# Key weights of a graph attention layer: 13 bursts of 768 columns a head over six PSUM banks, instead of 20 bursts of 475 or 494 over four

## The chip, the cores and the metric

One core of a Trainium2 chip runs the kernel. It has a matrix engine (PE, with its weight loads listed apart as PEld), three elementwise engines (DVE, ACT, POOL), a queue engine (SP) that issues most DMAs, an on-chip memory SBUF of 128 partitions, and a matmul memory PSUM of eight banks, each 128 partitions by 512 f32. The metric is device time in microseconds (us). All arithmetic here is in f32.

## The reference

A layer of two-direction graph attention over B = 16 batches of N = 512 nodes with F = 512 features, H = 16 heads of dh = 32, and only the first NG = 20 nodes as keys. Cut to what matters:

```python
vcq = concatenate([v, where(row_zero, 0, q)])          # (16, 512, 1024)
self_feat = vcq @ W_self.T + b_self                    # (16, 512, 512)
output = self_feat
for d in range(2):                                     # adjacency, and its transpose
    A = (adj if d == 0 else swapaxes(adj, 1, 2))[:, :, :20, :]
    cond, vb = A.sum(-1), A @ w_bias + b_bias          # 11 labels
    kv = self_feat[:, :20]
    qh = (self_feat @ Wq[d].T + bq[d]).reshape(B, N, 16, 32)
    kh = (kv @ Wk[d].T + bk[d]).reshape(B, 20, 16, 32)
    aff = einsum('bnhd,bmhd->bnhm', qh, kh) / sqrt(32)
    w = softmax(where(cond > 0, aff, -9e15) + vb)      # over the 20 keys
    out_t = einsum('bnhm,bmf->bnhf', w, kv)
    output += einsum('bnhf,hgf->bnhg', out_t, Wout[d]) + bout[d]
return v + relu(output)
```

## The kernel before, in words

The kernel never forms `qh`. Scores of a batch are one product of `self_feat` with **key weights** g: for each head and key, Wq of that head times the key's row. A softmax doesn't change when one key's score is taken from all of them, so only ND = 19 differences of keys are kept for each batch, direction and head. The program has a setup (everything for all 16 batches that depends on the keys), a loop over batches from L1085, and a tail from L1293.

**Setup.** Self features of the keys come first (L781), their differences `kvD` (L821, on DVE) and key rows `khD` (`key_rows`, matmul L838, then L847 on DVE), one for each direction d and group hg of four heads. Then come the **bursts** (`keys`, matmul L937). A unit is one batch of 19 columns, for a block fc of 128 features, a group hg, a direction d. A burst takes 26 or 25 units in order, so 494 or 475 columns, and cuts them into runs wherever fc, hg or d changes. Each run is one matmul for each of the four heads hl of the group. Such a matmul contracts over the 32 rows of its head, so the four heads sit in four row groups of the array and run side by side. Each head has a PSUM bank of its own: heads 0 and 1 in the pair of banks s0, heads 2 and 3 in the pair s1. ACT empties s0 (L959) and DVE s1 (L961), one instruction for a run, both with the scale, into stage tiles `st` (one per fc and hg: 128 by batch, head, direction, key). When a stage tile is full, POOL copies batch 0 into `g0` (L965), which the loop's first batch reads, and SP stores the other 15 batches to `g_d` in DRAM (L968). The loop reads a batch's key weights back with four loads (`load_keys`).

Between two bursts PE works on **fillers**, so that ACT and DVE have time to empty the banks. A string `plan` (L990) says which fillers follow which burst: `v` and `w` (`values`, L900, products of key features with Wout), `c` (`bias_scores`, L873), `n` (`row_flags`, L220, which rows are zero), `p` (`block_product`, L282, the first batch's self features); `m` and `b` are work for DVE and ACT. Early bursts have `key_rows` there instead. Fillers use a rotating pool of four banks, s0 and s1 the other four. Each engine runs its own instructions in the order in which the program is written.

**Loop.** For each batch, halves, directions and row blocks go through `score_product` (L395), mask and softmax (ACT, DVE, POOL: `weigh`, `lowered`, `total`, `normal`), a transpose (`turn`, DVE L543) and `attend` (L567 on PE). `normal` multiplies by the reciprocal sum (POOL L535), `key_sum` forms differences of key weights for products that serve several blocks (POOL L368), `apart` builds a part of the values (POOL L167), `mask_spread` and `mask_count` prepare masks (L344, L331).

Of the kernel before, what the change touches and what calls it, by code (L numbers as in the profile page):

```python
# [7 lines left out]
F32 = mybir.dt.float32  # L8
# [5 lines left out]
P = 128  # L14
# [4 lines left out]
def gat_kernel(  # L19
# [47 lines left out]
    def bank(name):  # L67
        return acc["pool"].tile([P, 512], F32, tag="acc", name=name)
# [10 lines left out]
    g0 = const.tile([P, C, WD], F32, tag="g", name="g0")  # L79
# [7 lines left out]
    g_d = dram.tile([C * C, P, B - 1, WD // C], F32, name="g_d")  # L87
# [44 lines left out]
    def load_keys(b, ks=range(C), ins=None):  # L132
        if ks[0] == 0:
            gs[b] = (gp if b % 2 else const).tile([P, C, WD], F32, tag="g", name=f"g{b}", bufs=1)
        src = g_d[:, :, b - 1]
# [81 lines left out]
    def row_flags(b):  # L217
        ps = bank(f"ps_nz{b}")
        for a in range(HL):
            nc.tensor.matmul(ps[bass.ts(a, R), :N], ones[:, :R], rss[b], start=True, stop=True)  # L220
        nzs[b] = load.tile([P, N], F32, tag="nz", name=f"nz{b}")
        nc.vector.tensor_scalar(nzs[b], ps[:, :N], 0.0, None, ALU.not_equal)
# [34 lines left out]
    def product(b, n):  # L257
# [13 lines left out]
        if first:  # L271
            parts[b, home] = bank(f"ps_{home}{b}")
# [424 lines left out]
    with tc.tile_pool(name="setup", bufs=1) as sp, tc.tile_pool(name="ps_acc", bufs=4, space=PSUM) as acc["pool"]:  # L697
        wq_sb = sp.tile([P, 2, C, F], F32, name="wq_sb")
        wo_sb = sp.tile([P, 2, C, F], F32, name="wo_sb")
# [16 lines left out]
        with tc.tile_pool(name="setup_k", bufs=1) as sk:  # L716
# [17 lines left out]
            warm = bank("ps_warm")  # L734
# [32 lines left out]
            nc.sync.dma_start(bb_sb, b_bias.partition_broadcast(P))  # L767
            for d in range(2):
                rows(wo_sb[:, d], woT[d])
            load_x(1)  # L770
            load_adj(0, 1)
# [5 lines left out]
            kv_ps = [bank(f"ps_kv{fc}") for fc in range(C)]  # L777
# [32 lines left out]
            for fc in range(C):  # L810
# [11 lines left out]
                    kvD[:, fc].rearrange("p (b m) -> p b m", m=ND), each[:, :, 1:],  # L822
# [8 lines left out]
            def key_rows(d, jc, ks=range(C)):  # L831

                if ks[0] == 0 and (d, jc) not in of:
                    of[d, jc] = bank(f"ps_k{d}{jc}")
# [32 lines left out]
        with tc.tile_pool(name="setup_g", bufs=3) as sg:  # L867

            def bias_scores(d):

                ps = bank(f"ps_c{d}")
                for c in range(C):
# [7 lines left out]
                    ps[:, : B * ND].rearrange("p (b m) -> p b m", m=ND),  # L880
# [10 lines left out]
            def values(t, ds, k):  # L891
# [3 lines left out]
                if k == 0:  # L895
                    held[1 + t // 2] = bank(f"ps_v{t}{ds[0]}")
                ps = held[1 + t // 2]
                for i, d in enumerate(ds):
                    for a in range(rows // R):
                        nc.tensor.matmul(  # L900
                            ps[bass.ds(i * rows + a * R, R)], kvT[:, k, bass.ds(t * P + a * R, R)], wo_sb[:, d, k],
# [26 lines left out]
            def keys(runs):  # L928


                pairs = [ps_s.tile([P, 2, 512], F32, tag=f"s{i}", name=f"ps_g{runs[0]}{i}", bufs=1) for i in range(2)]
                at = 0
                for fc, hg, d, lo, hi in runs:
                    n = (hi - lo) * ND
                    for hl in range(HL):
                        r = bass.ts(hl, DH)
                        nc.tensor.matmul(  # L937
                            pairs[hl // 2][:, hl % 2, at : at + n], wq_sb[r, d, hg, bass.ts(fc, P)],
                            khD[r, d * C + hg, lo * ND : hi * ND], start=at == 0, stop=True, skip_group_check=True,
                        )  # L940
                    at += n
                if not units and runs is bursts[-1]:
                    for hl in range(HL):
                        r = bass.ts(hl, DH)
                        nc.tensor.matmul(
                            pairs[hl // 2][:, hl % 2, at:], wq_sb[r, 0, 0, :P], khD[r, 0, : 512 - at],
                            start=False, stop=True, skip_group_check=True,
                        )
                at = 0
                for fc, hg, d, lo, hi in runs:  # L950
                    n = (hi - lo) * ND
# [10 lines left out]
                    at += n  # L962
                    if d == 1 and hi == B:
                        to, of = g0[:, fc, bass.ts(hg, WD // C)], st[:, 0].rearrange("p h d m -> p (h d m)")
                        nc.gpsimd.tensor_copy(to, of)  # L965
                        to, of = g_d[C * fc + hg], st[:, 1:].rearrange("p b h d m -> p b (h d m)")
                        most = fc * hg < (C - 1) * (C - 1)
                        nc.sync.dma_start(*((to, of) if most else (to[:, :1], of[:, :1])))  # L968
# [25 lines left out]
            while units:  # L994
                runs = []
                for fc, hg, d, b in units[: 25 + (len(bursts) % 5 < 3)]:
                    if runs and runs[-1][:3] == (fc, hg, d):
                        runs[-1] = (*runs[-1][:4], b + 1)
                    else:
                        runs.append((fc, hg, d, b, b + 1))  # L1000
                del units[: 25 + (len(bursts) % 5 < 3)]
                bursts.append(runs)
            rest = [(d, hg) for hg in range(C) for d in range(2)]
            first = None
# [8 lines left out]
            for n, runs in enumerate(bursts):  # L1013
                for i in range(len(rest)):
                    if (i < 1 and n > 0) or any(fc == 0 and (d, hg) == rest[0] for fc, hg, d, _, _ in runs):
                        key_rows(*rest.pop(0))
                if n in (3, 4):
                    values(*steps["v"].pop(0)[1])
                if n == 0:
                    bo_rows = load.tile([P, C, N], F32, tag="x2", name="bo_rows", bufs=1)  # L1020
                    nc.sync.dma_start(bo_rows[:, :2], bout.partition_broadcast(P))
                keys(runs)
                if n == 8:
                    mask_count(0, 0)
                if n == 14:
                    mask_count(0, 1)
                if n == 17:
                    mask_sum(0, 1)
                value_pieces()
                if rest:  # L1030
                    for kind in "mm" if n else ():
                        f, args = steps[kind].pop(0)
                        f(*args)
                    continue
                if n == 7:
                    mask_mul(0, 0)
                first = n if first is None else first
# [395 lines left out]
```

## Time and profile before

| what | value |
|---|---|
| median of 3 runs | 547.67 us (547.23 to 548.54) |
| the profiled execution | 547.91 us |
| span of its trace | 546.2 us |
| first burst, first score product of the loop | 24.26 us, 89.17 us |
| POOL, DVE, ACT busy, share of the span | 82%, 88%, 74% |

A row of the timeline or the groups reads: start and duration in us, or a count, then engine, line and operation, output <- inputs, partitions x elements. `32*128` before a matmul's shape is the part of the array it uses, rows times columns. An f32 matmul leaves two records, one for each of two passes. The profile's span is 1.7 us shorter than the time of the execution that it belongs to.

### The profile page before, as it was taken

How to read it: one execution, taken by the hardware profiler on the slowest of the kernel's cores; microseconds unless marked ns; L12 is line 12 of the kernel's file. 1: busy time of each engine (PE TensorE's matmuls, PEld its weight loads, DVE VectorE, ACT ScalarE, POOL GpSimd, SP SyncE). 2: the span in 40 equal slices, each digit the busy share in tenths (PEclk: the TensorE clock that was granted, in tenths of full speed). 3: DMA queues.
4: the chain of work that ended last, by engine and by line, in shares of the span. 5: the costliest groups of instructions: out<-in, count | busy, mean ns of one | idle time of the engine just before them, and what ended most of it. 6: DMA issues, size and time to landing. Idle time of an engine off the chain costs nothing.

```text
span 546.2 us, 19863 instructions
## 1 busy us (share of the span) xinstructions
PE 539.6 (99%) x8012; PEld 421.6 (77%) x8012; DVE 481.3 (88%) x716; ACT 404.6 (74%) x1000; POOL 449.5 (82%) x454
## 2 busy tenths in 40 slices
PE   8999999999999999999999999999999999999996
PEld 5544368889788878787888878888878788878784
DVE  1776678889999999999999999999998999999997
ACT  1225445888787979788888888888878887978564
POOL 2647995779989897979898989898998989797675
PEclk9999999999999999999999999999999999999998
DMA  8999899967676777787776867676777776736025
GB/s 312 378 401 347 280 370 359 321 193 215 200 223 181 226 204 208 240 214 227 214 215 188 229 186 214 212 199 216 193 240 191 219 211 184 233 95 192 2 65 195
DMA packets 96715, 122.80 MB, mean 225 GB/s; under 512 B 19264, under 2 KB 65022, under 8 KB 94576
## 3 DMA queue, kind: packets, MB, share of 16 engines
q1 hardware_dynamic: 95200, 119.18, 70.6%
q0 software_dynamic: 992, 1.57, 1.4%
q8 instruction: 63, 1.03, 0.8%
q10 hardware_dynamic: 432, 0.79, 0.4%
q14 instruction: 28, 0.23, 0.1%
HBM read 84.66 MB, written 38.15 MB: 225 GB/s over the span
## 4 chain that ended last, share of the span: by engine, by line
PE 90%; DVE 3%; DMA 2%; ACT 2%; POOL 1%; issue 1%; DVEq 0%; ACTq 0%; POOLq 0%
PE ps_f L665 29%; PE ps_a L395 22%; PE ps_c L395 10%; PE ps_d L395 6%; PE ps_o_f L567 5%; PE ps_v L900 3%; PE ps_k L838 3%; PE ps_kv L781 2%; PE ps_a L282 1%; PE ps_o_c L567 1%; PE ps_l L395 1%; DMA nz_d<-nz 1%; DMA nz<-nz_d 1%; PE ps_c L282 1%; DMA ws_v<-in_wsT 1%; DVE sm L530 1%
## 5 line engine op out<-in xcount | busy, mean ns | idle before, releaser
L325 ACT ACTIVATE prod<-adj,wb_sb 128x80 f32<-128x80 int32 x330 | 116.1, 430 | 0.0
L535 POOL TENSOR_TENSOR w<-w,sm 128x640 f32<-128x640 f32 x63 | 80.4, 1276 | 30.9 <-DVE sm L531 27.5
L665 PE MATMUL ps_f<-t,ws_s 128*64 128x246 f32 x720 | 80.0, 370 | 0.0
L665 PEld LDWEIGHTS ps_f<-t,ws_s 128*64 128x64 f32 x720 | 51.7, 136 | 18.9
L526 ACT ACTIVATE w<-w 128x640 f32<-128x640 f32 x60 | 43.9, 731 | 18.5 <-DVE w L522 18.5
L543 DVE STREAM_TRANSPOSE wt<-w 128x640 f32<-128x640 f32 x63 | 52.5, 834 | 0.9 <-POOL w L535 0.8
L665 PE MATMUL ps_f<-x,ws_v 128*64 128x246 f32 x480 | 52.4, 371 | 0.0
L530 DVE TENSOR_REDUCE sm<-w 128x32 f32<-128x640 f32 x63 | 51.1, 811 | 1.2 <-ACT w L526 1.0
L521 DVE TENSOR_REDUCE ps_d<-w 128x32 f32<-128x640 f32 x59 | 48.7, 826 | 1.8 <-ACT ps_d L429 0.2
L522 DVE TENSOR_TENSOR w<-w,ps_d 128x640 f32<-128x640 f32 x59 | 48.4, 821 | 2.0
L665 PEld LDWEIGHTS ps_f<-x,ws_v 128*64 128x64 f32 x480 | 34.7, 137 | 13.0
L368 POOL TENSOR_TENSOR k<-g,k 128x608 f32<-128x608 f32 x30 | 44.6, 1488 | 0.0
L395 PEld LDWEIGHTS ps_a<-g,sf 128*64 128x64 f32 x544 | 34.2, 137 | 5.9 <-issue 5.8
L395 PE MATMUL ps_a<-g,sf 128*64 128x152 f32 x544 | 38.6, 295 | 0.0
L395 PE MATMUL ps_d<-g,sf 128*64 128x152 f32 x544 | 37.9, 293 | 0.0
L336 DVE TENSOR_REDUCE add<-prod 128x80 f32<-128x960 f32 x32 | 36.7, 1146 | 0.8 <-POOL prod L331 0.7
L344 ACT COPY both<-add 64x80 f32<-64x80 f32 x128 | 32.7, 255 | 5.7 <-DVE add L336 4.6
L567 PE MATMUL ps_o_c<-wt,ve 32*32 32x256 f32 (+1 forms) x480 | 35.9, 386 | 0.0
L680 POOL TENSOR_TENSOR t<-x,t 128x492 f32<-128x492 f32 x30 | 34.8, 1160 | 1.2
L395 PEld LDWEIGHTS ps_d<-g,sf 128*64 128x64 f32 x544 | 35.3, 137 | 0.2 <-ACT sf L683 0.2
L680 POOL TENSOR_TENSOR t<-x 128x492 f32<-128x492 f32 x30 | 34.5, 1150 | 0.0
L197 ACT ACTIVATE xn<-xn 128x512 f32<-128x512 f32 x56 | 34.5, 619 | 0.0
(308 smaller groups left out, 1487.7 us busy)
## 6 DMA issues: line engine op xcount, KB each, us to landing
g<-g_d SPq DMA_DIRECT2D x60, 304.0 KB, 3.1
g_d<-st SPq DMA_DIRECT2D x15, 1140.0 KB, 8.2
out_T<-o SPq DMA_DIRECT2D x64, 256.0 KB, 3.3
x<-in_xT SPq DMA_DIRECT2D x56, 256.0 KB, 4.3
xn<-in_xn SPq DMA_DIRECT2D x48, 256.0 KB, 5.4
adj<-in_adj SPq DMA_DIRECT2D x52, 220.0 KB, 3.6
nz<-nz_d SPq DMA_DIRECT2D x14, 256.0 KB, 5.3
adj<-in_adj SPq DMA_DIRECT2D x6, 440.0 KB, 5.8
```

Source lines behind the costliest of these rows:

```text
L325: nc.scalar.activation(p[:, :, l], a[:, :, l], AF.Identity, scale=wb_sb[:, l : l + 1])
L368: done["ksum"] = engine.tensor_sub(to, one, two)
L395: nc.tensor.matmul(slot(g)[bass.ts(p, P // 2), : HL * S].rearrange("p (h m) -> p h m", m=NG)[:, :, 1:], of(k)[:, bass.ds(first + g * P // ...
L521: nc.vector.tensor_reduce(mx, f, AX.X, ALU.max)
L522: done["weigh"] = (engine or nc.vector).tensor_sub(f, f, mx.unsqueeze(2).to_broadcast([P, per, NG]))
L526: done["exp"] = nc.scalar.activation(t, t, AF.Exp)
L530: nc.vector.tensor_reduce(sm, heads(weighs[b, c, l]), AX.X, ALU.add)
L535: done["normal"] = nc.gpsimd.tensor_mul(f, f, smalls.pop((b, c, l)).unsqueeze(2).to_broadcast([P, per, NG]))
L543: done["turn"] = nc.vector.transpose(wts[b][:, c, l], weighs.pop((b, c, l)).rearrange("p g w -> p (g w)"))
L567: nc.tensor.matmul(outsum[b][a][bass.ds(at // 2 * DH, n * DH), bass.ds(c * N // 2 + lo * R, (hi - lo) * R)].rearrange("p (n r) -> p n r", ...
L665: nc.tensor.matmul(parts[b][n in (2, 3, 5)][bass.ts(a, P // 2), bass.ts(i, HN)], lhs, x[:, k], start=False, stop=k == 1, skip_group_check= ...
L680: done["xsum"] = nc.gpsimd.tensor_sub(to, one, two)
```

## The change

- **Units, bursts, banks.** A unit is now one key for all 16 batches: 16 columns of `khD`, whose columns are now ordered key first, batch second (`kvD` is written in that order, L821). A burst takes 48 units, 768 columns a head; there are 13 (the last has 32 units). The first 32 units fill the banks s0 and s1 as before. The other 16 ("more") go to a third tile `both` of two banks, t2: heads 0 and 1 share its first bank, 256 columns each, heads 2 and 3 its second. Fillers have two banks, acc0 and acc1.
- **Order in a burst.** Heads 0 and 2 begin with their runs in t2, heads 1 and 3 end with them. The second head of a bank waits for the first one's matmul.
- **Emptying.** ACT still takes the half of heads 0 and 1, DVE the other one, now of s0, s1 and of both banks of t2. The innermost loop of these instructions is the batch, which is the outermost in `st`, so consecutive elements lie 608 bytes apart (4 heads x 2 x 19 x 4 bytes); before, 19 consecutive elements lay side by side. The third tile is read by ACT and DVE in turns, as the second listing below shows.
- **Plan.** `plan` is new: up to three `v` after a burst. `values` and `row_flags` use 64-column tiles in place of 32-column ones, half the instructions. The extra matmuls L945 at the end of the last burst are gone.
- **Batch 1.** POOL copies batch 1 too, into `g1` (16 copies more); `g_d` has 14 batches, and the four loads of batch 1 are gone, as is the late store at L1141. The second half of Wout lies in the buffer that `ws_q` frees.
- **Loop, batch 1.** In that batch alone, `apart` comes earlier and one `key_sum` of batch 2 later.

```diff
-            def keys(runs):
-                pairs = [ps_s.tile([P, 2, 512], F32, tag=f"s{i}", name=f"ps_g{runs[0]}{i}", bufs=1) for i in range(2)]
+            def keys(n):
+                runs = bursts[n]
+                pairs = [ps_s.tile([P, 2, 512], F32, tag=f"s{i}", name=f"ps_g{n}{i}", bufs=1) for i in range(2)]
+                both = acc["pool"].tile([P, 2, 512], F32, tag="t2", name=f"ps_g{n}2") if n + 1 < len(bursts) else None
+                each = [sorted(runs, key=lambda run: hl % 2 == (run[5] > 0)) for hl in range(HL)]
+                gone = [0] * HL
+                while any(each):
+                    hl = min((hl for hl in range(HL) if each[hl]), key=lambda hl: gone[hl])
+                    fc, hg, d, lo, hi, more, at = each[hl].pop(0)
...
+                    to = both[:, hl // 2, bass.ds(hl % 2 * 256 + at, w)] if more else pairs[hl // 2][:, hl % 2, bass.ds(at, w)]
+                    if more and hl % 2 and at == 0:
+                        behind(nc.tensor.nop(), done["key", hl - 1])
...
-                        to = st[:, lo:hi, bass.ts(half, 2), d].rearrange("p b h m -> p h b m")
-                        of = pairs[half][:, :, at : at + n].rearrange("p h (b m) -> p h b m", m=ND)
+                        to = st[:, :, bass.ts(half, 2), d, lo:hi].rearrange("p b h m -> p h m b")
+                        of = both[:, half].rearrange("p (h w) -> p h w", h=2) if more else pairs[half]
+                        of = of[:, :, bass.ds(at, (hi - lo) * B)].rearrange("p h (m b) -> p h m b", b=B)
...
-            plan = "mmvv bvv vvc vvc vvn vvw vw vw wn p p p p p p p".split()
+            plan = "mm mmm mmmvvv vvv vvvb cvvv vvc vvn wwwn wp pp pp pp".split()
...
-            units = [(fc, hg, d, b) for fc in range(C) for hg in range(C) for d in range(2) for b in range(B)]
+            units = [(fc, hg, d, m) for fc in range(C) for hg in range(C) for d in range(2) for m in range(ND)]
...
-                    if d == 1 and hi == B:
-                        to, of = g0[:, fc, bass.ts(hg, WD // C)], st[:, 0].rearrange("p h d m -> p (h d m)")
-                        nc.gpsimd.tensor_copy(to, of)
+                    if d == 1 and hi == ND:
+                        for b in range(2):
+                            nc.gpsimd.tensor_copy(
+                                near[b][:, fc, bass.ts(hg, WD // C)], st[:, b].rearrange("p h d m -> p (h d m)")
+                            )
+                        nc.sync.dma_start(g_d[C * fc + hg], st[:, 2:].rearrange("p b h d m -> p b (h d m)"))
...
             if more:
-                at(further, key_sum, b + 1, 1)
+                at(b == 1, apart, 0)
+                at(b != 1 and further, key_sum, b + 1, 1)
                 mask_spread(b + 1, 0)
                 mask_count(b + 1, 1)
...
-            at(b == 1, apart, 0)
             total(b, 1, 1)
             at(0 < b and further, load_nz, b + 2, done["sum"])
             normal(b, 1, 1)
+            at(b == 1, key_sum, 2, 1)
```

On PE, the second burst before (`ps_g...0` and `...1` are the pairs s0 and s1; the last number of a shape is the columns of the run) was issued like this:

```order
L937 MATMUL ps_g(0, 0, 1, 10, 16)0_408<-khD_101,wq_sb_99 128x114 [waits PE_49,Activation_49]
L937 MATMUL ps_g(0, 0, 1, 10, 16)0_408<-khD_101,wq_sb_99 128x114
L937 MATMUL ps_g(0, 0, 1, 10, 16)1_409<-khD_101,wq_sb_99 128x114 [waits DVE_49,PE_49]
L937 MATMUL ps_g(0, 0, 1, 10, 16)1_409<-khD_101,wq_sb_99 128x114
L937 MATMUL ps_g(0, 0, 1, 10, 16)0_408<-khD_101,wq_sb_99 128x304 x2
L937 MATMUL ps_g(0, 0, 1, 10, 16)1_409<-khD_101,wq_sb_99 128x304 x2
L937 MATMUL ps_g(0, 0, 1, 10, 16)0_408<-khD_101,wq_sb_99 128x76 x2
L937 MATMUL ps_g(0, 0, 1, 10, 16)1_409<-khD_101,wq_sb_99 128x76 x2
```

The fourth burst after (numbered 3; `ps_g30` and `ps_g31` are the pairs, `ps_g32` is t2) begins like this:

```order
L943 MATMUL ps_g32_582<-khD_102,wq_sb_100 128x224 [waits DVE_49,PE_49]
L943 MATMUL ps_g30_580<-khD_102,wq_sb_100 128x128
L943 MATMUL ps_g32_582<-khD_102,wq_sb_100 128x224
L943 MATMUL ps_g31_581<-khD_102,wq_sb_100 128x128
L943 MATMUL ps_g30_580<-khD_102,wq_sb_100 128x304
L943 MATMUL ps_g31_581<-khD_102,wq_sb_100 128x304
L943 MATMUL ps_g32_582<-khD_102,wq_sb_100 128x32 x2
L943 MATMUL ps_g30_580<-khD_102,wq_sb_100 128x128
L943 MATMUL ps_g31_581<-khD_102,wq_sb_100 128x128
```

The first matmul of a burst now writes t2, and it is the one that waits for DVE; before, the first ones wrote the pairs and waited for ACT and for DVE, each for its own pair.

On ACT, the same burst is emptied with these five instructions:

```order
L958 ACTIVATE st03_556<-ps_g30_580 128x2x8x16 [waits PE_49]
L958 ACTIVATE st10_610<-ps_g30_580 128x2x19x16 [waits DMAHW3_49,Activation_49,Pool_49]
L958 ACTIVATE st10_610<-ps_g30_580 128x2x5x16
L958 ACTIVATE st10_610<-ps_g32_582 128x2x14x16 [waits PE_49]
L958 ACTIVATE st11_620<-ps_g32_582 128x2x2x16 [waits DMAHW4_49,DVE_49,Pool_49]
```

and on DVE with these:

```order
L960 TENSOR_SCALAR st03_556<-ps_g31_581 128x2x8x16 [waits PE_49]
L960 TENSOR_SCALAR st10_610<-ps_g31_581 128x2x19x16 [waits DMAHW3_49,Pool_49]
L960 TENSOR_SCALAR st10_610<-ps_g31_581 128x2x5x16
L960 TENSOR_SCALAR st10_610<-ps_g32_582 128x2x14x16 [waits Activation_49]
L960 TENSOR_SCALAR st11_620<-ps_g32_582 128x2x2x16 [waits DMAHW4_49,Activation_49]
```

Emptying the pairs needs no turn of the other engine. For t2, DVE's first piece waits for ACT's first, ACT's second for DVE's first, and DVE's second for ACT's second.

On POOL, these rows stood in the last part of batch 1 in the loop (the digit behind a letter is the batch: `k2_1` and `g2` are of batch 2, `w1_11` and `sm1_11` of batch 1, `ve0` and `vd0` the values of batch 0):

```order
L368 TENSOR_TENSOR k1_2_1486<-g1_1174,k1_2_1486 128x608
L368 TENSOR_TENSOR k2_1_1727<-g2_1490 128x608 [waits DMAHW7_49,DMAHW2_49,PE_49]
L331 TENSOR_SCALAR prod2_1_1672<-cond2_1_1733 128x80 [waits DVE_49]
L167 TENSOR_TENSOR ve0_1740<-vd0_1577,own_85 128x192 [waits DMAHW5_49,DMAHW6_49,DMAHW4_49,DMAHW3_49]
L167 TENSOR_TENSOR ve0_1740<-vd0_1577,own_85 128x192
L535 TENSOR_TENSOR w1_11_1660<-w1_11_1660,sm1_11_1743 128x640 [waits DVE_49,Activation_49]
```

and after the change these:

```order
L368 TENSOR_TENSOR k1_2_1520<-g1_85,k1_2_1520 128x608
L167 TENSOR_TENSOR ve0_1761<-vd0_1611,own_86 128x192 [waits DMAHW2_49,DMAHW7_49,DMAHW1_49,DMAHW0_49]
L167 TENSOR_TENSOR ve0_1761<-vd0_1611,own_86 128x192
L331 TENSOR_SCALAR prod2_1_1706<-cond2_1_1768 128x80 [waits DVE_49]
L535 TENSOR_TENSOR w1_11_1694<-w1_11_1694,sm1_11_1775 128x640 [waits DVE_49,Activation_49]
L368 TENSOR_TENSOR k2_1_1781<-g2_1524 128x608 [waits DMAHW6_49,DMAHW3_49,PE_49]
```

The row `k2_1` has moved from ahead of `w1_11` to behind it, and the two rows `ve0` stand ahead of `prod2_1`.

More of the change, by code (lines that the diff above doesn't have):

```diff
@@ L217, in row_flags @@
     def row_flags(b):
-        ps = bank(f"ps_nz{b}")
-        for a in range(HL):
-            nc.tensor.matmul(ps[bass.ts(a, R), :N], ones[:, :R], rss[b], start=True, stop=True)
+        ps = bank(f"ps_nz{b}", 1)
+        for a in range(2):
+            nc.tensor.matmul(ps[bass.ts(a, P // 2), :N], ones[:, : P // 2], rss[b], start=True, stop=True)
         nzs[b] = load.tile([P, N], F32, tag="nz", name=f"nz{b}")
@@ new lines, in keys @@
+            def keys(n):
[7 more added lines that the diff above has]
+                    fc, hg, d, lo, hi, more, at = each[hl].pop(0)
+                    r, w = bass.ts(hl, DH), (hi - lo) * B
+                    gone[hl] += w
+                    to = both[:, hl // 2, bass.ds(hl % 2 * 256 + at, w)] if more else pairs[hl // 2][:, hl % 2, bass.ds(at, w)]
+                    if more and hl % 2 and at == 0:
+                        behind(nc.tensor.nop(), done["key", hl - 1])
+                    one = nc.tensor.matmul(
+                        to, wq_sb[r, d, hg, bass.ts(fc, P)], khD[r, d * C + hg, lo * B : hi * B],
+                        start=at == 0 and not (more and hl % 2), stop=True, skip_group_check=True,
+                    )
+                    if more:
+                        done["key", hl] = one
+                for fc, hg, d, lo, hi, more, at in runs:
@@ L1163, in gat_kernel @@
                 total(b, 0, 0)
-                at(more, load_keys, b + 1, range(2, 3), done["sum"])
+                at(one and more, load_keys, b + 1, range(2, 3), done["sum"])
                 normal(b, 0, 0)
@@ L1173, in gat_kernel @@
                 normal(1, 0, 0)
-            at(more, load_keys, b + 1, range(3, 4), done["sum" if b == 1 else "lowered"])
+            at(one and more, load_keys, b + 1, range(3, 4), done["sum" if b == 1 else "lowered"])
             at(two, turn, b - 1, 0, 1)
```

174 lines of the change are left out of this document (70 added, 104 removed).

## The prediction

> **What bounds the kernel now.** I read the head of the page first, then the slices, then the chain that ended last.
>
> ```profile
> span 546.2 us, 19863 instructions
> PE 539.6 (99%) x8012; PEld 421.6 (77%) x8012; DVE 481.3 (88%) x716; ACT 404.6 (74%) x1000; POOL 449.5 (82%) x454
> PE   8999999999999999999999999999999999999996
> PEclk9999999999999999999999999999999999999998
> PE 90%; DVE 3%; DMA 2%; ACT 2%; POOL 1%; issue 1%; DVEq 0%; ACTq 0%; POOLq 0%
> ```
>
> PE is busy 99% of the span, at full clock in nearly every slice, and holds 90% of the chain. So time goes only if PE gets less work or loses a gap, and time comes whenever another engine makes PE wait. Next I cut the span into the stretch of the bursts and the loop's batches 0 to 2.
>
> ```profile
> 24.30:89.20 64.90, 64.87 (x841) 33.91 (x838) 46.59 (x92) 28.09 (x67) 45.71 (x64) 1.00 0.98 350
> 89.20:115.30 26.10, 26.10 (x337) 22.49 (x338) 22.96 (x27) 19.98 (x52) 22.37 (x20) 1.00 0.80 275
> 115.30:144.80 29.50, 29.41 (x434) 25.26 (x430) 27.55 (x41) 25.38 (x64) 26.14 (x26) 1.00 0.80 230
> 144.80:173.40 28.60, 28.60 (x440) 23.60 (x432) 26.97 (x39) 24.37 (x63) 25.72 (x25) 1.00 0.71 209
> ```
>
> Columns: window, length, then busy time of PE, PEld, DVE, ACT, POOL, then clock, DMA share, GB/s. In the stretch of the bursts PE never waits (64.87 of 64.90), so nothing is hidden there for the change to uncover: it can only shorten PE's work, or break a cover that holds today. Batch 1 is 0.9 us longer than batch 2, and 0.09 of it is idle time.
>
> **The change part by part.** First PE's work in the setup. The first row below is the same cut for the lines of the bursts alone, the others are PE's timeline (start, length):
>
> ```profile
> 24.20:89.20 65.00, 23.12 (x384) 15.76 (x384) 1.00 0.98 350
> ...
> 43.02 1.92 PE L900 MATMUL ps_v<-wo_sb,kvT 128*32 128x512 f32 x16
> 44.87 0.37 PE L937 MATMUL _g(1, 0, 1, 10, 16)0_609<-khD,wq_sb 32*128 32x114 f32 x2
> ...
> 45.99 1.92 PE L900 MATMUL ps_v<-wo_sb,kvT 128*32 128x512 f32 x16
> ...
> 83.09 0.28 PE L937 MATMUL g(3, 2, 0, 14, 16)0_1047<-khD,wq_sb 32*128 32x38 f32 x2
> ...
> 83.20 0.50 PE L937 MATMUL g(3, 2, 0, 14, 16)0_1047<-khD,wq_sb 32*128 32x304 f32 x2
> ```
>
> The 20 bursts are 23.12 us busy, their overlapping ends counted; from start to start, as in 44.87 to 45.99, one takes 1.01 to 1.18, and 20 take 21.9. The columns are 9728 a head (12 x 494 + 8 x 475). A column costs 1.67 ns in two passes: a burst of 304 + 190 columns without a short run takes 1.05 = 0.82 + 0.22 of switching. 9728 columns take 16.2 us, before and after. A short pass does not shrink with its columns: the pass of 38 columns takes 83.20 - 83.09 = 0.11, where its columns alone would take 0.03. Runs under 134 columns lose about 0.11 - 0.83 ns x columns in each pass. Before there are 16 of these, 1.2 us lost in all; 16.2 + 1.2 + 20 x 0.22 = 21.8 checks. After there are 22, of 16 to 128 columns, 1632 together: 22 x 0.224 - 1632 x 1.67 ns = 2.2 us. So 13 bursts take 16.2 + 2.2 + 13 x 0.22 = 21.3, with the dummy matmuls L945 gone: **-0.5 us**. A filler stretch has such a cost too:
>
> ```profile
> 56.87 2.78 PE L900 MATMUL ps_v<-wo_sb,kvT 128*32 128x512 f32 x24
> 59.58 0.53 PE L937 MATMUL s_g(2, 0, 0, 0, 16)0_773<-khD,wq_sb 32*128 32x304 f32 x2
> ```
>
> Three `v` take 59.58 - 56.87 = 2.71, two take 44.87 - 43.02 = 1.85; so one is 0.86 and each stretch has 0.14 on top. Seven stretches fewer: **-1.0 us**. The 64-column tiles of `values` I cost at nothing: the 32-column ones run side by side in the array (4 of them, 0.86 us), and half as many of double width fill it the same way. If tiles of 64 columns did not, the 16 `v` and 4 `w` would grow; nothing in the rows speaks for it, since L282 uses 64-column tiles and keeps PE full.
>
> Next, the cover. PE may start a burst when its banks are empty.
>
> ```profile
> 43.24 1.08 ACT L959 ACTIVATE st<-s_g(1, 0, 0, 0, 16)0_576 128x608 f32<-128x608 f32 x2 [1.98 <-POOL g L965]
> 43.35 1.25 DVE L961 TENSOR_SCALAR st<-s_g(1, 0, 0, 0, 16)1_577 128x608 f32<-128x608 f32 x2 [0.54 <-PE s_g(1, 0, 0, 0, 16)1_577 L937]
> L959 ACT ACTIVATE st<-_g(0, 0, 1, 10, 16)0_408 128x608 f32<-128x608 f32 x1 | 0.7, 693 | 0.0
> L959 ACT ACTIVATE st<-_g(0, 0, 1, 10, 16)0_408 128x152 f32<-128x152 f32 x1 | 0.3, 303 | 0.0
> L961 DVE TENSOR_SCALAR st<-_g(0, 0, 1, 10, 16)1_409 128x608 f32<-128x608 f32 x1 | 0.8, 782 | 0.0
> L961 DVE TENSOR_SCALAR st<-_g(0, 0, 1, 10, 16)1_409 128x152 f32<-128x152 f32 x1 | 0.3, 306 | 0.0
> ```
>
> That burst ended at 43.02; ACT began 0.22 later, and both engines had emptied the banks by 44.60, before PE's next burst at 44.87. Now ACT costs about 0.17 us + 0.86 ns an element of a partition (303 at 152, 693 at 608), DVE 0.15 + 1.04 ns. After the change a burst has 1024 elements in the pairs and 512 in t2 for each engine. On ACT the pairs end 0.22 + 1.12 = 1.34 after the burst (1.08 for 988 elements, so 1.12 for 1024). DVE empties its pair beside that. Then come the turns in t2: ACT, DVE, ACT, DVE. They are two ACT pieces, 2 x 0.17 + 512 x 0.86 ns = 0.78, two DVE pieces, 2 x 0.15 + 512 x 1.04 ns = 0.83, and four hand-overs of 0.02 to 0.1: together some 1.8. So the next burst may start **3.1 to 3.3 us** after the last one; I take 3.2. Where DVE has a `v` to add first it is later still. If the two engines needed no turns, each would be done by about 2.2.
>
> The cover after the change, by the plan, in the same rows and these:
>
> ```profile
> 25.30 2.25 PE L838 MATMUL ps_k<-kvD,wk 128*32 128x304 f32 x32
> ...
> 48.46 0.46 PE L937 MATMUL s_g(1, 1, 1, 4, 16)0_655<-khD,wq_sb 32*128 32x228 f32 x2
> ...
> 53.14 1.92 PE L900 MATMUL ps_v<-wo_sb,kvT 128*32 128x512 f32 x16
> 54.88 1.04 PE L220 MATMUL ps_nz<-rx,ones 128*32 128x512 f32 x8
> 55.85 0.41 PE L937 MATMUL s_g(1, 3, 0, 7, 16)0_739<-khD,wq_sb 32*128 32x171 f32 x2
> 78.28 1.88 PE L282 MATMUL ps_a<-t,ws_s 128*64 128x246 f32 x16
> ...
> 80.10 0.46 PE L937 MATMUL _g(3, 1, 1, 4, 16)0_1015<-khD,wq_sb 32*128 32x228 f32 x2
> ```
>
> `vvn` covers 55.85 - 53.14 = 2.71, `p` 80.10 - 78.28 = 1.82, so `wp` 0.86 + 1.82 = 2.7 and `pp` 3.5; `vvv` covers 2.71; `vvc` is the least, as before 45.99 to 48.46, 2.47. Behind bursts 0 and 1 stand two `key_rows` each (2 x 2.2, L838). So PE waits about 0.5 behind bursts 2, 3, 4, 7 and 9, 0.7 behind 6, and not behind 5, 8, 10, 11: **+3.2 us**. The waits stand at the head of PE's queue, so all fillers and the loop behind them move by as much.
>
> POOL gets 16 copies more:
>
> ```profile
> L965 POOL COPY g<-st 128x152 f32<-128x152 f32 x16 | 5.8, 369 | 12.8 <-ACT st L959 7.2 <-DVE st L961 5.6
> L331 POOL TENSOR_SCALAR prod<-cond 128x80 f32<-128x80 f32 x32 | 18.1, 565 | 8.3 <-DVE cond L330 6.6
> ```
>
> They cost 16 x 0.37 = 5.9 us on an engine that is busy 45.71 of these 64.90. POOL also builds inputs of `p`, and now seven `p` stand behind four bursts instead of seven. I put **+0.5 us** there (between 0, if they fit in its idle time, and 5.9, if all of it came late). The dropped store and loads of batch 1 take DMA traffic away (share 0.98 in this stretch); no PE wait hung on it, so nothing for that.
>
> Last, the loop's batch 1, in the chain of waits:
>
> ```profile
> 137.42 0.57 POOL prod L331
> ...
> 138.07 0.98 POOL ve L167 x2
> 139.05 1.24 POOL w L535
> ...
> 140.32 0.85 DVE wt L543
> ...
> 142.40 0.40 PE ps_o_f L567
> ```
>
> PE's `attend` at 142.40 hung on DVE's transpose, that on POOL's `w`, and that on POOL's row ahead of it. The change puts the `key_sum` of batch 2 (1.5 us, L368, before 137.42) behind `w`. Then `w` comes up to 1.5 us earlier; DVE, in order, is free for the transpose 0.8 earlier. Batch 1 exceeds batch 2 by 0.9, so I take **-0.7 us** (between 0 and -0.9). Next in line is DVE's own work.
>
> Sum against the profiled execution: 547.9 - 0.5 - 1.0 + 3.2 + 0.5 - 0.7 = **549.4**. That execution is 0.2 over the median shown, so a median may come 0.2 lower.
>
> **The price of the stride.** The emptying now writes elements 608 bytes apart. No row of ACT or DVE before shows that from PSUM; the nearest by kind is L959 itself, and the sum takes its rate. The other bound is a row that steps through SBUF, reading every 44 and writing every 48 bytes, beside one that does neither:
>
> ```profile
> L325 ACT ACTIVATE prod<-adj,wb_sb 128x80 f32<-128x80 int32 x330 | 116.1, 430 | 0.0
> L344 ACT COPY both<-add 64x80 f32<-64x80 f32 x128 | 32.7, 255 | 5.7 <-DVE add L336 4.6
> L626 ACT ACTIVATE ps_f<-nz,qw x30: 469/470/472, 90.0 to 491.1; 128x246 f32<-128x246 f32 x30
> ```
>
> L325 takes 430 ns against 255. Some 90 is its scale from memory (L626, with one too, takes 470 at 246 elements, where 0.17 + 0.86 ns gives 0.38). The other 85 over 80 elements is 1.1 ns each: the rate about halved. Read or write, the row does not tell. The Trainium skill, "SBUF — State Buffer", in the box on SBUF cachelines in the section "Door 1: The DMA port swizzle", says that memory lines are 16 bytes and that an access to a new line each time pays a penalty, four f32 being free; L325 agrees, but its read steps too. By that page the sum would be that of the rival below.
>
> **The rivals.** *Half rate.* If the stride doubles the time of an element, the chain of 3.2 grows by 1024 x 0.86 on ACT's pairs, 512 x 0.86 and 512 x 1.04 in t2: 1.8, so 5.0. Against covers of 2.5 to 3.6, ten waits sum to 20, the first two to 1; with -1.5 and -0.7 that is **567**. For it speaks L325, and L331 above, which writes every 48 bytes and takes 565 on POOL for 80 elements; against it, that L325 also reads with a step. Half of that surcharge gives 557.
> *It fits (the other side).* If the turns overlap, or a DVE or ACT piece starts while the other still reads, the banks are empty by 2.2 to 2.6 and no wait is left: 547.9 - 1.5 - 0.7 = **545.7**. It decides at 2.7, the length of `vvv`. For it: today's emptying has a margin, 44.60 against 44.87. Against it: the waits in the program name the other engine at each piece of t2.
> *Only half of it.* With waits of 0.2 in place of 0.5 and no late POOL, the parts cancel: 547.9 - 1.5 + 1.4 - 0.7 = **547.1**.
>
> **How the numbers follow.** The forecast, turns at full rate, gets 0.38 (own range 548.3 to 551.5), of which 0.05 lies under the bound; half rate or part of it 0.27 (556 to 567.5); all hidden 0.25 (545 to 546.4); cancelled 0.1. A measurement of this kernel can tell about 0.2%, 1.1 us, from no change. So faster 0.27 (all hidden, with some of the cancelled), same 0.13, slower 0.6. The range is 545.2 to 567: hidden at its low end, the doubled stride at its upper one.
>
> **What would show it.** The rows of L958 and L960: 0.69 and 0.78 us for 608 elements at full rate, 1.2 and 1.4 at half. In the timeline, PE idle ahead of L943, released by DVE, about 0.5 us, behind the bursts named. In t2 the pieces ACT, DVE, ACT, DVE one after another. PE's time from first burst to first score product: 64.9 before, about 67 if I am right, 63.4 if all is hidden, 84 at half rate. Batch 1 of the loop 28.8 in place of 29.5. Wrong would I be if pieces of t2 run side by side, or if the chain is under 2.7.

## The result

The changed kernel takes 588.71 us (median of 4 runs, 587.45 to 589.84), the kernel before 547.53 us in the same runs: a ratio of 1.075, 95% interval 1.0733 to 1.0766. It is slower, as forecast, but by 41 us and not by 2, and the time lies above the range given (545.2 to 567.0).

The head of the page of the changed kernel, and its slices:

```profile
span 585.7 us, 19799 instructions
PE 549.8 (94%) x7980; PEld 433.5 (74%) x7980; DVE 507.0 (87%) x724; ACT 434.6 (74%) x1008; POOL 452.2 (77%) x470
PE   9975686779999999999999999999999999999995
PEclk9989978989999999999999999999999999999998
```

PE has fallen from 99% to 94%, and only in slices 3 to 9. In the same slices the granted clock drops to seven to nine tenths. The first score product of the loop now starts at 128.1 us in place of 89.2, so 38.9 us of the 39.5 by which the span grew lie ahead of it.

The stretch of the bursts, cut as before (window, length, busy time of PE, PEld, DVE, ACT, POOL, then clock, DMA share, GB/s):

```profile
24.60:128.30 103.70, 75.44 (x811) 43.61 (x809) 74.00 (x100) 58.38 (x75) 50.47 (x83) 0.90 0.67 235
```

It was 64.90 long with 64.87 of PE. So PE now waits 103.70 - 75.44 = 28.3 us, and is busy 10.6 us longer, at a mean clock of 0.90: e4 below does the same work in 65.70 us at full clock. What PE waited for there (total, times, longest):

```profile
PE ps_g L943 <- DVE st L960: 21.7, 9, 3.2
PE ps_g L943 <- DVE khD L847: 3.0, 2, 2.1
PE ps_a L282 <- DVE sf L295: 2.9, 1, 2.9
PE ps_c L873 <- ACT bqbd L863: 0.7, 1, 0.7
```

The waits are of the kind that the prediction named, ahead of the bursts and for DVE. But there are nine of 1.8 to 3.2 us, 21.7 in all, where it had six of 0.5 to 0.7, 3.2 in all, and they stand behind bursts 5, 8 and 10 too, where it had none. The other three are work of DVE or ACT that stands in their queues behind the emptying. The groups of the emptying, by shape (busy, mean ns, idle before):

```profile
L958 ACT ACTIVATE st<-ps_g 128x608 f32<-128x608 f32 x8 | 14.1, 1762 | 6.7 <-PE ps_g L943 6.7
L958 ACT ACTIVATE st<-ps_g 128x32 f32<-128x32 f32 x2 | 0.6, 313 | 1.4 <-DVE st L960 1.4
...
L960 DVE TENSOR_SCALAR st<-ps_g 128x608 f32<-128x608 f32 x8 | 13.6, 1705 | 1.0 <-PE ps_g L943 1.0
...
L960 DVE TENSOR_SCALAR st<-ps_g 128x32 f32<-128x32 f32 x2 | 0.5, 232 | 0.3 <-ACT st L958 0.3
```

608 elements take 1762 ns on ACT and 1705 on DVE; they took 693 and 782. From 32 to 608 elements that is (1762 - 313) / 576 = 2.5 ns an element on ACT and (1705 - 232) / 576 = 2.6 on DVE, where 0.86 and 1.04 held before.

One burst, number 2, in the timelines of PE, ACT and DVE:

```profile
41.42 1.85 PE L943 MATMUL ps_g<-khD,wq_sb 32*128 32x80 f32 x32 [0.82 <-DVE khD L847]
43.20 2.80 PE L900 MATMUL ps_v<-wo,kvT 128*64 128x512 f32 x12
49.21 1.92 PE L943 MATMUL ps_g<-khD,wq_sb 32*128 32x224 f32 x40 [3.21 <-DVE st L960]
...
43.29 3.08 ACT L958 ACTIVATE st<-ps_g 128x576 f32<-128x576 f32 x3 [2.74 <-PE ps_g L943]
46.99 1.03 ACT L958 ACTIVATE st<-ps_g 128x352 f32<-128x352 f32 x1 [0.62 <-DVE st L960]
...
46.40 0.55 DVE L960 TENSOR_SCALAR st<-ps_g 128x160 f32<-128x160 f32 x1 [0.21 <-ACT st L958]
48.05 1.02 DVE L960 TENSOR_SCALAR st<-ps_g 128x352 f32<-128x352 f32 x1 [1.10 <-ACT st L958]
```

The burst ends at 43.20. ACT empties its pair and its first piece of t2 until 46.37, DVE takes a piece from 46.40, ACT one from 46.99, DVE the last from 48.05 to 49.07, and PE goes on at 49.21: 6.0 us after the burst, with 2.8 us of cover. The turns are as forecast; the pieces are too long.

### The profile page after: what moved, and what is told of

The parts are those of the page before. It is cut to its first block, busy times and chain, and to the rows that moved or that the text cites. A ratio compares the mean times of both kernels' runs of the same rounds, so it can differ in the third digit from the quotient of the medians.

```text
span 585.7 us, 19799 instructions
## 1 busy us (share of the span) xinstructions
PE 549.8 (94%) x7980; PEld 433.5 (74%) x7980; DVE 507.0 (87%) x724; ACT 434.6 (74%) x1008; POOL 452.2 (77%) x470
## 3 DMA queue, kind: packets, MB, share of 16 engines
q1 hardware_dynamic: 93088, 116.69, 63.4%
## 4 chain that ended last, share of the span: by engine, by line
PE 76%; DVE 2%; ACT 1%; issue 0%; DVEq 0%
PE ps_f L665 30%; PE ps_a L395 22%; PE ps_c L395 11%; PE ps_d L395 6%; PE ps_o_f L567 5%; PE ps_o_c L567 1%; PE ps_l L395 1%; PE ps_a L282 1%; PE ps_o_s L567 0%; ACT st L958 0%; DVE o L609 0%; DVE w L463 0%; PE ps_c L282 0%; DVE mx L461 0%; ACT w L466 0%
## 5 line engine op out<-in xcount | busy, mean ns | idle before, releaser
L325 ACT ACTIVATE prod<-adj,wb_sb 128x80 f32<-128x80 int32 x330 | 116.0, 429 | 0.0
L958 ACT ACTIVATE st<-ps_g 128x608 f32<-128x608 f32 (+18 forms) x56 | 51.9, 1086 | 45.0 <-PE ps_g L943 34.5
L960 DVE TENSOR_SCALAR st<-ps_g 128x608 f32<-128x608 f32 (+18 forms) x56 | 53.5, 1028 | 28.2 <-ACT st L958 18.1
L943 PE MATMUL ps_g<-khD,wq_sb 32*128 32x304 f32 (+18 forms) x448 | 25.9, 365 | 24.6 <-DVE st L960 21.7
L943 PEld LDWEIGHTS ps_g<-khD,wq_sb 32*128 32x128 f32 x448 | 22.3, 200 | 33.3 <-issue 30.8
L336 DVE TENSOR_REDUCE add<-prod 128x80 f32<-128x960 f32 x32 | 36.6, 1144 | 1.6 <-POOL prod L331 1.4
```

The lines of the kernel that those rows point to most:

```text
L325: nc.scalar.activation(p[:, :, l], a[:, :, l], AF.Identity, scale=wb_sb[:, l : l + 1])
L943: one = nc.tensor.matmul(to, wq_sb[r, d, hg, bass.ts(fc, P)], khD[r, d * C + hg, lo * B : hi * B], start=at == 0 and not (more and hl % 2) ...
L958: nc.scalar.activation(to, of, AF.Copy, scale=SCALE)
L960: nc.vector.tensor_scalar(to, of, SCALE, None, ALU.mult)
```

## The experiments

Ten kernels ran, in three groups; the kernel before, run again in each group, gave 547.59, 547.66 and 547.97 us. Of e8 and e9 only the durations of single instructions count, and each has one execution.

**e1: runs of neighbours are written, the step goes to the reading side.**

```diff
-                        to = st[:, :, bass.ts(half, 2), d, lo:hi].rearrange("p b h m -> p h m b")
+                        to = st[:, :, bass.ts(half, 2), d, lo:hi].rearrange("p b h m -> p h b m")
...
-                        of = of[:, :, bass.ds(at, (hi - lo) * B)].rearrange("p h (m b) -> p h m b", b=B)
+                        of = of[:, :, bass.ds(at, (hi - lo) * B)].rearrange("p h (m b) -> p h b m", b=B)
```

> The changed kernel, but each instruction that empties the banks loops over the key innermost: it writes runs of up to 19 neighbouring elements and reads PSUM with a step of 64 bytes. Theory S (the price lies in writing SBUF with a 608-byte step): the 608-element rows fall from 1.76 us on ACT and 1.71 on DVE to about 0.7 and 0.8, PE's waits ahead of the bursts from 2 to 3 us each to about 0.5, and the time to 547 to 551. Rival R (a step costs the same on the reading side): the rows stay near 1.7 us and the time near 588.

552.12 us, ratio 1.0086 (1.0071 to 1.0101). The same eight instructions of ACT, in its groups:

```profile
L958 ACT ACTIVATE st<-ps_g 128x608 f32<-128x608 f32 x8 | 5.5, 692 | 6.7 <-DMA adj<-in_adj 6.7
```

692 ns in place of 1762: the order of the loop in the writing instruction costs 588.7 - 552.1 = 36.6 us, and a step of 64 bytes in reading PSUM costs nothing. The time is 1 us above what theory S named.

**e2: the same turns, written side by side.** It leaves out the right order of the key weights and shows the prediction's own case.

```diff
-                        to = st[:, :, bass.ts(half, 2), d, lo:hi].rearrange("p b h m -> p h m b")
+                        flat = st.rearrange("p b h d m -> p (b h d m)").rearrange("p (h d m b) -> p h d m b", h=HL, d=2, b=B)
+                        to = flat[:, bass.ts(half, 2), d, lo:hi]
```

> The changed kernel, emptying the same banks in the same instructions and turns, but each writes its elements side by side (to places of the stage tile that aren't the right ones, so the key weights are permuted and the output isn't the reference's). It shows the turns at full rate, which the forecast of 549.4 assumed. Theory S: rows of 0.70 and 0.78 us for 608 elements, chain from a burst's end to the next burst 3.1 to 3.3 us, waits of about 0.5 us behind six bursts, 549 to 550. Rival T (the turns of ACT and DVE in t2, not the rate, make the loss): waits of 2 us and more remain and the time is above 570.

551.88 us, 1.0079 (1.0064 to 1.0094). The timelines of ACT, DVE and PE behind burst 3, which ends at 43.66:

```profile
43.64 1.59 ACT L959 ACTIVATE st<-ps_g 128x256 f32<-128x256 f32 x4 [2.53 <-PE ps_g L943]
45.97 0.23 ACT L959 ACTIVATE st<-ps_g 128x64 f32<-128x64 f32 x1 [0.74 <-issue]
...
45.26 0.62 DVE L961 TENSOR_SCALAR st<-ps_g 128x448 f32<-128x448 f32 x1 [0.23 <-ACT st L959]
46.23 0.23 DVE L961 TENSOR_SCALAR st<-ps_g 128x64 f32<-128x64 f32 x1 [0.34 <-ACT st L959]
...
46.60 1.69 PE L943 MATMUL ps_g<-khD,wq_sb 32*128 32x64 f32 x32
```

The next burst starts 46.60 - 43.66 = 2.94 us after the last one: the forecast said 3.1 to 3.3. Behind bursts 2, 4, 6 and 7 it is 2.9 to 3.0 us as well. At full rate the turns are thus priced rightly, a little high. Behind bursts 8 and 9 it is 4.1 and 3.8 us: there an ACT piece waits for POOL's copy out of a stage tile first (1.6 and 0.8 us), which the forecast's chain doesn't have. Yet the time is 2.5 us above the forecast of 549.4; e4 shows why.

**e3: no turns.** The third tile becomes two of one bank each.

```diff
-                both = acc["pool"].tile([P, 2, 512], F32, tag="t2", name=f"ps_g{n}2") if n + 1 < len(bursts) else None
+                both = [acc["pool"].tile([P, 512], F32, tag=f"t2{i}", name=f"ps_g{n}{2 + i}") for i in range(2)] if n + 1 < len(bursts) else None
...
```

> The changed kernel with the third tile split into two of one bank, one read by ACT alone and one by DVE alone: no turns, the stride stays. Theory S: rows stay at 1.76 and 1.71 us for 608 elements; 1536 elements on ACT take about 4.6 us, so the next burst may start 4.8 us after the last one in place of 6.0, waits fall by 1.2 us on ten bursts and some of the slow clock goes: 570 to 576. Rival T (turns are the loss): under 555.

560.53 us, 1.0235 (1.022 to 1.025): 28 us faster than the changed kernel, 10 more than theory S named, though each element still costs 2.5 ns. Its cut and its waits:

```profile
24.00:101.00 77.00, 67.15 (x810) 40.60 (x806) 68.21 (x100) 55.78 (x75) 49.51 (x81) 1.00 0.86 306
```

```profile
PE ps_g L943 <- ACT st L958: 8.3, 9, 1.4
```

The waits ahead of the bursts fall from 21.7 to 8.3 us, about the 12 that the expectation named. With none over 1.4 us the clock stays at 1.00, and PE's busy time falls from 75.44 to 67.15. The expectation had left that part almost out.

**e4: both edits.**

> Both edits: runs of neighbouring elements are written, and ACT and DVE take no turns. Theory S: emptying ends about 2.0 to 2.3 us after a burst, under every cover of 2.5 to 3.6, so PE waits for no burst: 545 to 546.5, which would beat the kernel before. Rival R: 570 to 576, as with two tiles alone.

550.24 us, 1.0049 (1.0032 to 1.0065). Not 545 to 546.5: with neither stride nor turns the change still loses 2.7 us. Its cut and its waits:

```profile
23.90:91.40 67.50, 65.70 (x807) 38.80 (x805) 46.71 (x100) 28.45 (x75) 48.86 (x80) 1.00 0.94 342
```

```profile
PE ps_a L282 <- POOL t L255: 1.3, 1, 1.3
PE ps_g L943 <- ACT st L958: 0.5, 1, 0.5
```

Waits are 1.8 us, and PE's own work is 65.70 where 63.4 was forecast and 64.87 stood before. From start to start its 13 bursts take 23.3 us, the 20 before took 21.9: the forecast was 21.3.

**e5: e4, and the sums that block_product reads come ahead of POOL's mask work.**

```diff
                     load_cq(0)
-                    mask_mul(0, 1)
                     new_self(0)
                     for i in range(1, 5):
                         x_sum(0, i)
+                    mask_mul(0, 1)
```

> The kernel of e4 (runs of neighbours written, two tiles in t2), and POOL builds the sums of x that block_product needs (L255) ahead of its 2.1 us of mask work (L322), as they come late for PE there: in e4 PE waited 1.3 us for them. Theory P (that order alone costs it): the wait of 1.3 goes and 548.7 to 549.2 is left of 550.2. Rival (POOL is full there whatever its order): the wait turns up elsewhere and the time stays 549.8 to 550.5.

549.13 us, 1.0027 (1.0018 to 1.0036). The wait for POOL is gone from the trace, and 1.1 us with it, as theory P said.

**e6: the kernel before, with the moved lines of the loop alone** (the last part of the diff of the change).

> The kernel before, with nothing changed but the three moved lines of the loop's batch 1 (apart earlier, one key_sum later). In the traces batch 1 went from 29.48 to 29.08 us with the change. Theory: the moved lines did that alone, so 0.4 us faster than before, 547.1 to 547.3. Rival: it came from the loads of batch 1 that are gone, and the time is that of before.

547.21 us, 0.9991 (0.9982 to 1.0000), with runs of 546.29 to 548.40. The times alone barely tell it from the kernel before. The traces do: the first score product of batch 1 and that of batch 2, in this kernel,

```profile
115.45 0.43 PE L395 MATMUL ps_a<-g,sf 128*64 128x152 f32 x4
...
144.50 0.48 PE L395 MATMUL ps_a<-g,sf 128*64 128x152 f32 x4
```

are 29.05 us apart. In the kernel before they stand at 115.32 and 144.80, 29.48 apart, in the changed one at 154.23 and 183.31, 29.08. So the moved lines gain 0.4 us, and the loads that are gone have no part in it. All traces without these lines (before, e8, e9) show 29.48, and those with them 29.05 to 29.11, but for e7, where batch 1 takes 29.42; why is open. e6 is the one version here whose median lies under that of the kernel before, and its interval reaches 1.0000.

**e7: the changed kernel with more work for PE.** In `values`, each matmul gets a partner with zero weights that accumulates into the same columns.

```diff
-                        nc.tensor.matmul(
-                            ps[bass.ds(i * rows + a * P // 2, P // 2)], kvT[:, k, bass.ds(t * P + a * P // 2, P // 2)], wo_sb[d][:, k],
-                            start=(k == 0), stop=(k == C - 1),
-                        )
+                        for real in (True, False) if k == 0 else (False, True):
+                            nc.tensor.matmul(
+                                ps[bass.ds(i * rows + a * P // 2, P // 2)],
+                                kvT[:, k, bass.ds(t * P + a * P // 2, P // 2)] if real else zero, wo_sb[d][:, k],
+                                start=(k == 0 and real), stop=(k == C - 1 and real),
+                            )
...
```

> The changed kernel (stride and turns kept), with one matmul of zero weights added to each matmul of values, accumulating nothing: 2.6 us more of PE work behind most bursts, which fills the time in which PE waits. The result is the same. Theory C (PE's granted clock falls because it waits, and 10 to 12 us of the 39 are that): the granted clock in the setup goes from 0.90 to 0.97 or more, waits ahead of the bursts shrink, and the kernel gets faster by 5 to 11 us with more work, 578 to 584. Rival (the clock has nothing to do with the waits): 588 to 592.

584.68 us, 1.0682 (1.0666 to 1.0698): 4.0 us faster than the changed kernel with some 17 us of matmuls more. Its cut:

```profile
24.40:124.80 100.40, 86.40 (x890) 48.43 (x886) 73.87 (x100) 57.79 (x75) 48.86 (x81) 0.97 0.68 240
```

The clock rises to 0.97, as theory C said, but the gain is 4 and not 5 to 11. Burst 7 in PE's timeline of the changed kernel and, behind it, of e7:

```profile
81.38 2.82 PE L943 MATMUL ps_g<-khD,wq_sb 32*128 32x192 f32 x40 [1.82 <-DVE st L960]
```

```profile
80.72 1.89 PE L947 MATMUL ps_g<-khD,wq_sb 32*128 32x192 f32 x40 [1.58 <-DVE st L964]
```

Bursts 4 and 9 differ likewise (2.23 and 2.42 us against 1.70 and 1.88), and so does the first `block_product` behind the last burst (3.56 against 1.90): 3.7 us together, close to the gain. They lie where nothing hides them. The rest of the slow work, fillers beside the emptying, only shortened PE's wait: from burst to burst the two kernels differ by 0.3 us at most elsewhere.

**e8 and e9: the price of a step by itself.** ACT, then DVE, write or read small pieces at the start of the kernel before.

```diff
+            nc.scalar.activation(flat[:, : 192 * 4].rearrange("p (n s) -> p n s", s=4)[:, :, 0], src, AF.Copy, scale=SCALE)
...
+            nc.scalar.activation(flat.rearrange("p (b m) -> p m b", b=16)[:, :12], two, AF.Copy, scale=SCALE)
```

> The kernel before, with 22 small instructions more at its start that ACT and DVE run one by one: 192 elements written from PSUM to SBUF with steps of 4, 8, 12, 16, 32, 48 and (as 12 x 16) 608 bytes, then read from SBUF with steps of 4, 8, 16 and 48 bytes and written side by side. Only the durations matter. Theory S: writing costs about 0.9 and 1.0 ns an element on ACT and DVE up to a step of 8 or 12 bytes and 2.5 ns from 16 bytes on, so rows of 0.33 to 0.36 us and of 0.62 to 0.66 us, and reading costs nothing at any step. Rival: the price grows with the step, 48 bytes being cheaper than 608.

ACT's timeline in e8, with steps of 4, 8, 12, 16, 32, 48 and 608 bytes in writing (L732 to L738), and of 4 and 16 bytes in reading SBUF (L739, L741):

```profile
4.96 0.33 ACT L732 ACTIVATE khD<-ps_q 128x192 f32<-128x192 f32 x1 [2.88 <-DVE khD L729]
5.33 0.34 ACT L733 ACTIVATE khD<-ps_q 128x192 f32<-128x192 f32 x1
5.70 0.43 ACT L734 ACTIVATE khD<-ps_q 128x192 f32<-128x192 f32 x1
6.16 0.51 ACT L735 ACTIVATE khD<-ps_q 128x192 f32<-128x192 f32 x1
6.70 0.51 ACT L736 ACTIVATE khD<-ps_q 128x192 f32<-128x192 f32 x1
7.24 0.50 ACT L737 ACTIVATE khD<-ps_q 128x192 f32<-128x192 f32 x1
7.78 0.65 ACT L738 ACTIVATE khD<-ps_q 128x192 f32<-128x192 f32 x1
8.45 0.36 ACT L739 ACTIVATE kvT<-khD 128x192 f32<-128x192 f32 x1
...
9.25 0.54 ACT L741 ACTIVATE kvT<-khD 128x192 f32<-128x192 f32 x1
```

Up to 8 bytes a step is free; from 16 to 48 bytes the 0.17 us added over 192 elements double the rate's price, by 0.9 ns an element; 608 bytes add 0.31 us, or 1.6 ns. DVE shows the same (0.36, 0.49 and 0.63 us). ACT has finished before DVE starts here, so the price doesn't come from both writing at once. Theory S is wrong twice: it gave 16 to 48 bytes the whole price of 608, and reading SBUF with 16 bytes costs ACT 0.18 us too. The rival, that the price grows with the step, needed e9:

> As e8, 180 elements in 12 rows of 15, written from PSUM with steps of 4 bytes (rows one behind the other) and of 48, 64, 128, 256, 480, 512, 544, 600, 608, 616 and 640 bytes. In e8 16 to 48 bytes cost 0.51 us for 192 elements and 608 bytes 0.65. Theory L (every step of 64 bytes or more pays the second surcharge): all from 64 bytes on take 0.60 to 0.63 us, 48 bytes 0.48. Rival B (it depends on which banks of the memory a step hits, so on multiples): 512 and 640, perhaps 608, are dearer than 600 and 616. Rival F (it is the 12 short rows): 4 and 48 bytes are dearer here too.

Rows of e9 by line (ns min/median/max), for 48, 256, 600, 608, 616 and 640 bytes:

```profile
L732 ACT ACTIVATE khD<-ps_q x1: 483/483/483, 5.3 to 5.3; 128x180 f32<-128x180 f32 x1
...
L735 ACT ACTIVATE khD<-ps_q x1: 472/472/472, 6.8 to 6.8; 128x180 f32<-128x180 f32 x1
...
L739 ACT ACTIVATE khD<-ps_q x1: 572/572/572, 8.9 to 8.9; 128x180 f32<-128x180 f32 x1
L740 ACT ACTIVATE khD<-ps_q x1: 572/572/572, 9.5 to 9.5; 128x180 f32<-128x180 f32 x1
L741 ACT ACTIVATE khD<-ps_q x1: 513/513/513, 10.1 to 10.1; 128x180 f32<-128x180 f32 x1
L742 ACT ACTIVATE khD<-ps_q x1: 472/472/472, 10.6 to 10.6; 128x180 f32<-128x180 f32 x1
```

None of the three theories holds, nor does e8's rival of a price that grows with the step. 48 to 640 bytes cost the same, 0.47 to 0.50 us, but for 600 and 608 (0.57) and 616 (0.51); DVE agrees. The step of this kernel is one of the two dearest tried. Why is open. A stage tile padded to 640 bytes a batch would test it in place; that was not tried.

**e10: e5, with one value product between the key rows and burst 2.** Its first value tile is read before `bout` has been added to its bias row, so a part of `bout` is left out.

```diff
-            plan = "mm mmm mmmvvv vvv vvvb cvvv vvc vvn wwwn wp pp pp pp".split()
+            plan = "mm mmmv mmmvvv vvv vvvb cvv vvc vvn wwwn wp pp pp pp".split()
```

> The kernel of e5 with one of the value products moved from behind burst 5 to behind the key rows that precede burst 2. In e5 burst 2 takes 2.16 us and burst 4, of the same number of runs, 1.65. Theory K (burst 2 waits inside for the key rows that DVE has just to finish): burst 2 falls to about 1.7 and the time by 0.4 to 0.5, to 548.5 to 548.8. Rival (the burst is longer for its runs' sizes): it stays at 2.1 and the time near 549.1.

548.93 us, 1.0020 (1.0011 to 1.0030). Burst 2 in PE's timeline of e10 and, behind it, in that of e5:

```profile
36.88 1.72 PE L943 MATMUL ps_g<-khD,wq_sb 32*128 32x80 f32 x32
```

```profile
36.35 2.23 PE L943 MATMUL ps_g<-khD,wq_sb 32*128 32x80 f32 x32
```

The same matmuls take 0.5 us less when DVE has had time to finish the key rows, so theory K holds: in burst 2 PE waits inside a burst, where the views count it as busy. Burst 0 follows key rows too and takes 1.64 us to the next work in e5, so the change from key rows to a burst doesn't cost it. Against its own runs of before, e10 loses 0.2% and e5 0.27%; the times are too close to give the 0.4 by themselves.

## Why the prediction was wrong

The step that failed is **the price of the stride**: "the nearest by kind is L959 itself, and the sum takes its rate". It costs 2.5 ns an element on ACT and 2.6 on DVE in place of 0.86 and 1.04, so a burst is emptied in 6.0 us and not in 3.2. With 6.0 the prediction's own sum gives ten waits of 60 - 30 = 30 us, 3 behind the first two bursts, and 547.9 - 1.5 + 33 - 0.7 = 579.

- **The rival at half rate** had the mechanism and too small a size. It took its price, 0.9 to 1.0 ns more an element, from L325, which steps by 44 and 48 bytes; e8 confirms 0.9 for 16 to 48 bytes. At 608 bytes it is 1.6, which no row that the prediction shows could tell, and the range ended where L325's price ended. The Trainium skill, "SBUF — State Buffer", in the section "Door 1: The DMA port swizzle", puts the free step at four f32 and gives each new line of 16 bytes a penalty; e8 agrees that a new line each time costs, but not on the free step: 8 bytes are free (0.34 us), 12 bytes pay a part (0.43) and 16 bytes, four f32, the whole price (0.51). For 600 to 616 bytes that page has nothing.
- **PE's clock** stood in no rival. The rest between 579 and 589 is in part this: e7 gets 4.0 us back by keeping PE busy. The granted clock in the changed kernel, in windows behind waits of 2.2, 3.2 and 2.4 us (window, length, busy time, clock, DMA share, GB/s):

```profile
35.14:40.60 5.46, 5.46 (x65) 0.78 0.51 179
59.17:63.10 3.93, 3.90 (x15) 0.71 0.35 102
75.50:79.60 4.10, 4.06 (x18) 0.63 0.52 181
```

In e3, whose waits are 1.4 us at most, it stays at 1.00. The Trainium skill, "TensorE: Matmul & The Clock Gate", Part 1, lets the clock fall after a whole idle window of about 3.4 us; here it fell though no wait was longer than 3.21 us. It didn't fall behind every such wait: behind the longest one it was 1.00 (49.21 to 53.77 us), and behind 2.9 us of waiting for `sf` it was 0.50 in the changed kernel (122.87 to 126.17) but 1.00 in e7 (121.11 to 124.70). What decides is not shown. The remainder, 5 to 6 us, was taken apart only in part. The wait for `sf` is in it (2.9 us), and some 1.5 us more in the first two bursts (8.09 and 8.66 us from start to start, where 6.0 and a burst of 1.64 make 7.64). Against them, the last burst, which uses no t2, didn't wait, where the sum has 2.5 us (6.0 less a cover of 3.5).
- **The turns** were right in kind and size (2.94 measured against 3.1 to 3.3, e2). But turns and stride go together: at full rate the turns cost 552.1 - 550.2 = 1.9 us (e1 against e4), with the stride 588.7 - 560.5 = 28.2 us (the changed kernel against e3), the gain in clock included. The main sum took the turns at full rate; its rival did carry the stride through every turn.
- **PE's work** was mis-sized by 2.3 us (65.7 against 63.4, e4). The bursts take 23.3 and not 21.3. Some 0.9 of that lies in bursts 1 and 2, which need key rows just made (e10 shows it for burst 2, 0.5), the rest is about 0.1 a burst, not taken apart. By what is left of PE's work, fillers saved about half of the 1.0; perhaps because many `v` of before were followed by `c` or `n`, not by a burst, and had no cost of leaving to save, which was not tested. So "all hidden", 545.7, was not within reach: e4, where all but 0.5 us of the emptying is hidden, takes 550.24, and e5 without POOL's wait 549.13.
- **POOL** was right in kind: its wait is 1.3 us in e4, where 0.5 was taken, and e5 shows that the order of its work made it. In the changed kernel itself that wait doesn't appear.
- **The loop's batch 1** gained 0.4 us, not 0.7 (29.05 in place of 29.48, e6).
- From the first score product of the last batch to the end, the profiles of the changed kernel and its variants are 0.3 to 1.2 us longer than the four of the kernel before and its variants. The excess lies behind the last matmul, where the last output lands: 5.35 to 6.09 us against 4.89 to 5.10. Its cause stays open.

## What to carry to other kernels

Look at the innermost step of what is written to SBUF before counting instructions: here the order of one loop in two instructions cost 37 us, and the same data moved by stepping through PSUM instead cost none. Price such a step by a probe of that very step; a row with another step gave little more than half of it. Where waits in series pass through a slower instruction, its price counts once for every turn, and here waits of 2 to 3 us also took PE's clock down to 0.90 on average.

## What the runs showed of the hardware

- ACT and DVE write f32 to SBUF at full rate with steps of 4 and 8 bytes (0.33 and 0.34 us for 192 elements on ACT, e8), for 1.7 to 1.8 ns an element with 16 to 544 and with 640 bytes (0.50 to 0.51 us for 192, e8; 0.47 to 0.50 for 180, e9), and for 2.2 to 2.6 with 600 and 608 (0.57 us for 180, e9; 0.65 for 192, e8; 1762 ns for 608, the changed kernel). Both engines pay nearly the same (0.65 and 0.63 us at 608 bytes), though their rates without a step differ (0.86 and 1.04 ns).
- Reading PSUM with a step of 64 bytes is free (e1: 692 ns for 608 elements on ACT, 782 on DVE, as without a step), reading SBUF with 16 bytes isn't (e8: 0.36 to 0.54 us on ACT, 0.26 to 0.33 on DVE).
- Adding 17 us of matmuls to PE made a kernel 4 us faster (e7), with the clock at 0.97 in place of 0.90.
